# Pinning the layernorms of the first two sequences ahead of the sums, in a transformer block on one Trainium2 core

## Chip, core and metric

The kernel runs on one core of a Trainium2 chip. A core has five engines with their own instruction queues: TensorE (matmuls, "PE" in the profile), VectorE ("DVE"), ScalarE ("ACT"), GpSimd ("POOL") and SyncE ("SP", which here only starts DMAs). Each works through its queue in order and waits on semaphores for the others. The metric is the device time of one execution in microseconds (us), the median of several runs.

## What is computed

Sixteen sequences of 512 tokens with 256 features, all in float32. Each is layernormed; then linear attention with 16 heads and a mixture of experts are both applied to the normed tokens, and all is added to the input:

```python
xn = (x - mean) / sqrt(var + 1e-5)
q, k, v = xn @ Wq + bq, xn @ Wk + bk, xn @ Wv + bv
q, k = elu(q) + 1, elu(k) + 1
kv = einsum('bkhd,bkhm->bhdm', k, v)
attn = (q . kv) / max(q . sum(k), 1e-6) @ Wo + bo
shared = swiglu(xn @ w_in.T) @ w_out.T
h = swiglu(xn @ w1.T)
# 2 groups of 4 experts; softmax in the best group, two best experts e
routed = sum over the two: w_e * (h @ w2[e].T)
out = x + attn + shared + routed
```

## The kernel before

A sequence is four tiles of 128 tokens. For each sequence the kernel makes the layernorm `xn`, its transpose `xnT`, the keys together with the routing's logits (`pk`, 266 columns), the queries (`pq`), the feature maps of both, the sum of keys (`k2`, `ksb`), `pxk` (the product of normed tokens and keys, from which `mix` makes the attention's matrix `kvo`), the two SwiGLU hidden layers (`phr`, `hr` in token rows for the experts; `phs`, `hs` in columns for the shared part), and the output `po`. Sequence 0 computes the SwiGLU products directly (`first_rows`, `first_hidden`); the later ones with seven products in place of eight (`seven`). Rows for the experts go to DRAM (`h_d`). After the last sequence the tokens, sorted by pairs of experts, are read back by indirect DMAs and multiplied by the pair's weights (`Tiles`); this takes from about 792 us to the end.

The loop over sequences runs ahead: in the pass for sequence b, `front(b + 1)` computes keys, queries, feature maps and routing of b + 1, `normalize(b + 2)` the layernorm of b + 2, and `x` of b + 3 is loaded. Layernorms of sequences 0 and 1 are transposed on TensorE and copied out of PSUM by ScalarE; those of later sequences go through DRAM and VectorE's 32x32 transposes (`turn`, `qT` and `xnT`).

Three things set the order of the instructions. A scheduler puts each engine's instructions in an order by its own estimate of times. `tc.keep_in_program_order` (called `pin` in `first`) keeps an instruction in the order in which the program names it, among the pinned ones of its engine. `tc.issue_after(ins)` puts instructions of the same engine as `ins` behind it.

PSUM holds eight tiles: six of the pool `ps_mm` (tag `mm`: `pt`, `pk`, `pxk`, `phr`, `phs`, `pvk`, `pm`) and two of `ps_y` (`py`: the first queries, key sums, `po`). TensorE cannot begin a product until an earlier tile's slot was read and so freed, by VectorE or ScalarE. In both kernels the slot of `phs` of block 1 of sequence 0 is the one that `hr` of tile 1 frees.

Names and lines used below:

- L327 to L331: statistics, reciprocal and scale of sequence 0's layernorm (VectorE), L329 its Sqrt (ScalarE); L285 to L292 the same in `normalize`, for the others.
- L336/L339 and L302/L305: the transposes of sequences 0 and 1 on TensorE, and ScalarE's copies.
- L343: keys and queries of sequence 0; L404 and L415: keys and queries of the others. L369/L370 and L408/L409 add the biases to keys (`kk`) and logits (`lg`), L372 and L419 to queries (`qq`); the change calls the first pair `keep`.
- L382: `res`, the sums x + bo, on GpSimd; L668/L669: GpSimd's sum of keys; L507: `ahead_of`, its running counts for the routing.
- L389 to L394: the feature map (min, Exp, and the combining step on VectorE).
- L643, L661: the SwiGLU products of sequence 0 (`hr`, `hs_all`); L519: the weight sums made between them; L559 to L576: the seven-product form.
- L724 to L731: the normalizer `qk`, `rz`, and the scaled queries, stored to `q_d` (L736).
- L703/L708: `vk`; L713: `pm`.

Of the kernel before, what the change touches and what calls it, by code (L numbers as in the profile page):

```python
# [10 lines left out]
FP = mybir.dt.float32  # L11
AF = mybir.ActivationFunctionType
ALU = mybir.AluOpType
AX = mybir.AxisListType

P = 128
# [5 lines left out]
def block_kernel(  # L22
# [29 lines left out]
    nc = tc.nc  # L52
    B, S, D = x.shape
# [5 lines left out]
    KD = D // P  # L59
    KH = HID // P  # L60
    NT = S // P
# [22 lines left out]
    keep = ctx.enter_context(tc.tile_pool(name="keep", bufs=1))  # L84
    work = ctx.enter_context(tc.tile_pool(name="work", bufs=2))
    one = ctx.enter_context(tc.tile_pool(name="one", bufs=1))
    small = ctx.enter_context(tc.tile_pool(name="small", bufs=2))
    dram = ctx.enter_context(tc.tile_pool(name="dram", bufs=1, space=bass.MemoryType.DRAM))
    ps_mm = ctx.enter_context(tc.tile_pool(name="ps_mm", bufs=6, space=bass.MemoryType.PSUM))
# [10 lines left out]
    x_all, kk_all, qq_all, xn_all = (  # L100
        keep.tile([P, 2, NT, D], FP, name=f"{n}_all") for n in ("x", "kk", "qq", "xn")
    )
# [22 lines left out]
    eps_sb = const.tile([P, 1], FP)  # L125
    nc.gpsimd.memset(eps_sb, LN_EPS)
    ident = const.tile([P, P], FP)
    make_identity(nc, ident)

    xs = {0: load_x(0, NT)}  # L130
# [26 lines left out]
    for q in range(NQ):  # L157
        nc.gpsimd.dma_start(
            out=bv_sb[ts(q, Q)], in_=bv[ts(q, KD * Q)].rearrange("(c i) -> i c", i=Q)
# [22 lines left out]
    for k in range(KD):  # L182
        for c in range(KD):
            nc.sync.dma_start(
                out=wv_sb[:, k, ts(c, P)].rearrange("p (q i) -> p q i", i=Q), in_=by_quadrant(wv[ts(k, P), :])[:, c]
            )
    wo_sb = wp.tile([P, KD, D], FP)
    for q in range(NQ):
        nc.sync.dma_start(
            out=wo_sb[ts(q, Q)], in_=wo[ts(q, KD * Q), :].rearrange("(c i) d -> i c d", i=Q)  # L190
# [4 lines left out]
    def load_expert(i):  # L195
# [13 lines left out]
        out=headmask, in_=ones, pattern=[[-DH, P // DH], [0, DH]],  # L209
# [3 lines left out]
        out=headmask, in_=headmask, pattern=[[DH, P // DH], [0, DH]],  # L213
# [5 lines left out]
        out=before, in_=ones, pattern=[[1, P]],  # L219
# [3 lines left out]
    place = const.tile([P, NT * G, EG], FP)  # L223
# [28 lines left out]
    last_xn, last_copy = [], []  # L252
# [18 lines left out]
    def normalize(b):  # L271

        xt = xs[b]
        st = small.tile([P, NT, 6], FP, tag="st", name=f"st_{b}")
        mv = small.tile([P, NT, 2], FP, tag="mv", name=f"mv_{b}")
        sd = small.tile([P, NT], FP, tag="sd", name=f"sd_{b}")
        rs = small.tile([P, NT], FP, tag="rs", name=f"rs_{b}")
        xn = xn_all[:, b % 2]

        n = 1 if b == 0 else NT  # L280
        made = []
        for g in range(0, NT, n):
            with tc.issue_after(last_xn[-1].ins) if last_xn else nullcontext():
                for t in range(g, g + n):
                    nc.vector.bn_stats(out=st[:, t, :], in_=xt[:, t, :])  # L285
            for t in range(g, g + n):
                nc.vector.bn_aggr(out=mv[:, t, :], in_=st[:, t, :])
            with tc.issue_after(last_copy[-1].ins) if last_copy else nullcontext():
                nc.scalar.activation(sd[:, g : g + n], mv[:, g : g + n, 1], AF.Sqrt, bias=eps_sb)
            nc.vector.reciprocal(rs[:, g : g + n], sd[:, g : g + n])  # L290
            for t in range(g, g + n):
                made.append(nc.vector.tensor_scalar(  # L292
                    xn[:, t, :], xt[:, t, :], mv[:, t, 0:1], rs[:, t : t + 1],
                    ALU.subtract, ALU.mult,
                ))
        last_xn[:] = made[-1:]
        xnT = work.tile([P, KD, S], FP, tag="xnT", name=f"xnT_{b}")
        if b < 2:
            for t in range(NT):
                pt = ps_mm.tile([P, KD, P], FP, tag="mm", name=f"pt_{b}_{t}")  # L300
                for c in range(KD):
                    nc.tensor.transpose(  # L302
                        pt[:, c, :], xn[:, t, :].rearrange("p (m c) -> p c m", c=KD)[:, c], ident
                    )
                last_copy.append(nc.scalar.copy(xnT[:, :, ts(t, P)], pt))  # L305
            return xn, xnT, None
        last_copy.clear()
        nc.sync.dma_start(out=xn_d[b % 2].rearrange("(t p) d -> p t d", p=P), in_=xn)
        return xn, xnT, turn(xnT, xn_d[b % 2], "xb", b, "(i c)")

    def first():

        pin = tc.keep_in_program_order
        xt, xn, kk, qq = xs[0], xn_all[:, 0], kk_all[:, 0], qq_all[:, 0]
        st = small.tile([P, NT, 6], FP, tag="st", name="st_0")
        mv = small.tile([P, NT, 2], FP, tag="mv", name="mv_0")
        sd = small.tile([P, NT], FP, tag="sd", name="sd_0")  # L320
        rs = small.tile([P, NT], FP, tag="rs", name="rs_0")
        lg = small.tile([P, NT, E + G], FP, tag="lg", name="lg_0")
        xnT = work.tile([P, KD, S], FP, tag="xnT", name="xnT_0")
        pks, pqs = [], []

        def place(t):
            pin(nc.vector.bn_stats(out=st[:, t, :], in_=xt[:, t, :]))  # L327
            pin(nc.vector.bn_aggr(out=mv[:, t, :], in_=st[:, t, :]))
            pin(nc.scalar.activation(sd[:, t : t + 1], mv[:, t, 1:2], AF.Sqrt, bias=eps_sb))  # L329
            pin(nc.vector.reciprocal(rs[:, t : t + 1], sd[:, t : t + 1]))  # L330
            last_xn[:] = [pin(nc.vector.tensor_scalar(  # L331
                xn[:, t, :], xt[:, t, :], mv[:, t, 0:1], rs[:, t : t + 1], ALU.subtract, ALU.mult
            ))]
            pt = ps_mm.tile([P, KD, P], FP, tag="mm", name=f"pt_0_{t}")
            for c in range(KD):
                pin(nc.tensor.transpose(  # L336
                    pt[:, c, :], xn[:, t, :].rearrange("p (m c) -> p c m", c=KD)[:, c], ident
                ))
            last_copy[:] = [pin(nc.scalar.copy(xnT[:, :, ts(t, P)], pt))]  # L339

        def times(to, t, w):
            for k in range(KD):
                pin(nc.tensor.matmul(  # L343
                    to, lhsT=xnT[:, k, ts(t, P)], rhs=w[:, k, :], start=(k == 0), stop=(k == KD - 1)
                ))

        def keys(t):
            pks.append(ps_mm.tile([P, KR], FP, tag="mm", name=f"pk_0_{t}"))
            times(pks[t], t, wkr_sb)

        def queries(t):
            if t % 2 == 0:
                pqs.append(ps_y.tile([P, 2, D], FP, tag="py", name=f"pq_0_{t}"))
            times(pqs[-1][:, t % 2, :], t, wq_sb)

        place(0)
        place(1)
        keys(0)
        keys(1)
        queries(0)  # L360
        place(2)
        queries(1)
        keys(2)
        place(3)
        keys(3)
        queries(2)
        queries(3)
        for t in range(NT):
            pin(nc.vector.tensor_tensor(kk[:, t, :], pks[t][:, 0:D], bkr_sb[:, 0:D], ALU.add))  # L369
            pin(nc.vector.tensor_tensor(lg[:, t, :], pks[t][:, D:KR], bkr_sb[:, D:KR], ALU.add))  # L370
        for i, pq in enumerate(pqs):
            nc.vector.tensor_tensor(  # L372
                qq[:, 2 * i : 2 * i + 2, :], pq, bq_sb.unsqueeze(1).to_broadcast([P, 2, D]), ALU.add
            )
        return xn, xnT, (qq, kk, lg)

    def residual(b):

        res = work.tile([P, NT, BASE], FP, tag="res", name=f"res_{b}")
        xt = xs.pop(b)  # L380
        for t in range(NT):
            nc.gpsimd.tensor_tensor(res[:, t, 0:D], xt[:, t, :], bo_sb, ALU.add)  # L382
        return res

    def feature_map(b, y, tag):

        low = one.tile([P, NT, D], FP, tag="low", name=f"{tag}_{b}")
        if tag == "km":
            nc.vector.tensor_scalar(low, y, 0.0, None, ALU.min)  # L389
            nc.scalar.activation(low, low, AF.Exp)  # L390
        else:
            nc.scalar.activation(low, y, AF.Relu, scale=-1.0)
            nc.scalar.activation(low, low, AF.Exp, scale=-1.0)
        nc.vector.scalar_tensor_tensor(y, y, 0.0, low, ALU.max, ALU.add)  # L394

    def project(b, xnT):

# [582 lines left out]

    waiting = list(range(G * NL))

    *normed_0, (qq, kk, lg) = first()
    normed = {0: (*normed_0, None), 1: normalize(1)}
    res = residual(0)
    feature_map(0, kk, "km")
    feature_map(0, qq, "qm")
    route(0, lg, res)
    fronts = {0: (res, qq, kk)}
    queries = {}  # L990
    xs[2] = load_x(2)
    for b in range(B):
        xn, xnT, _ = normed.pop(b)
        res, qq, kk = fronts.pop(b)
        if b + 1 < B:
            fronts[b + 1] = front(b + 1, normed[b + 1][1])
        if b + 2 == B:

            nc.sync.dma_start(
                out=h_d[ts(b + 1, S), HID:ROW].rearrange("(t p) h -> p t h", p=P), in_=fronts[b + 1][0]  # L1000
# [43 lines left out]
    n = nc.values_load(  # L1044
        filled, min_val=TT, max_val=TILES,
        skip_runtime_bounds_check_because="whole tiles for all tokens, a part of a tile more for a pair",
    )
# [31 lines left out]
    for half, queue in enumerate((nc.sync, nc.scalar)):  # L1079
# [4 lines left out]
        for j in range(2):  # L1084
            t = 2 * half + j
# [36 lines left out]
```

## Time and profile before

| | |
|---|---|
| median of 3 runs | 1045.91 us (1045.9 to 1046.4) |
| the profiled execution | 1045.97 us; span from first to last instruction 1044.2 us |
| TensorE's mean granted clock | 0.992 |
| TensorE idle from 0 to 60 us | 10.4 us |
| TensorE idle from 60 to 735 us | 3.9 us |
| ScalarE: loads of an activation table | 46, at 1.28 us |

The profile is of one execution. Times in its rows are us from the start of the span, unless marked ns; "x4" counts instructions. In a row in order of time the first two numbers are start and duration, and a bracket at its end says how long the engine stood idle before it and what ended that. In a table of windows each engine has its busy time and number of instructions; after them stand TensorE's granted clock (1.00 is full speed), the share of the DMA engines, and GB/s. Matmuls overlap, so their starts, not their durations, give the pace. A float32 matmul of the program is two instructions on TensorE.

### The profile page before, as it was taken

The numbers are of one execution on the slowest core, as the hardware profiler recorded it, in microseconds if no ns is written. First come the engines' busy times: TensorE is split into PE (matmuls) and PEld (weight loads), VectorE is DVE, ScalarE is ACT, GpSimd is POOL, SyncE is SP. The second block draws the span as 40 slices with busy tenths as digits, with TensorE's granted clock in tenths as the row PEclk, the third lists the DMA queues.
The fourth block names the chain that finished last, engine by engine and source line by source line (L and its number), as shares of the span: only waits on it lengthen the run. The fifth ranks groups of instructions, "written<-read, shape, count | busy, mean of one in ns | idle before, by whom it ended". The sixth has DMA issues, their size and how long they took to land. (4 is left out here: it accounts for less than half of the span.)

```text
span 1044.2 us, 12410 instructions
## 1 busy us (share of the span) xinstructions
PE 1011.8 (97%) x3704; PEld 685.2 (66%) x3704; DVE 787.8 (75%) x1976; ACT 479.1 (46%) x886; POOL 242.3 (23%) x353
## 2 busy tenths in 40 slices
PE   6999999999999999999999999999896999999998
PEld 4566868677786868686777768686672444444445
DVE  5969797978788797878786877868975666666662
ACT  2415353534344352535344443425138666667770
POOL 5202020110202021110202020211022555565541
PEclk9999999999999999999999999999998999999999
DMA  7142624425151523314141313221253445544441
GB/s 217 42 138 87 174 87 116 127 71 151 51 161 49 162 78 87 121 42 141 41 121 56 115 57 114 84 61 61 60 141 127 142 137 154 160 149 149 149 125 69
DMA packets 130436, 114.24 MB, mean 109 GB/s; under 512 B 72605, under 2 KB 114589, under 8 KB 130368
## 3 DMA queue, kind: packets, MB, share of 16 engines
q1 hardware_dynamic: 120080, 77.42, 25.3%
q0 software_dynamic: 8912, 35.21, 11.2%
q10 hardware_dynamic: 1376, 0.80, 0.3%
q8 instruction: 31, 0.51, 0.2%
q14 instruction: 37, 0.30, 0.1%
HBM read 63.52 MB, written 50.27 MB: 109 GB/s over the span
## 5 line engine op out<-in xcount | busy, mean ns | idle before, releaser
L952 PE MATMUL py<-w_sb,hT 128*128 x536 | 233.1, 598 | 8.4 <-DMA w_sb<-in_w 8.4
L952 PEld LDWEIGHTS py<-w_sb,hT 128*128 128x128 f32 x536 | 102.7, 192 | 137.7 <-issue 137.7
L750 PE MATMUL po<-wout_sb,hs_all 128*128 128x256 f32 x512 | 124.9, 382 | 1.9 <-DVE hs_all L572 1.4
L382 POOL TENSOR_TENSOR res<-x_all,bo_sb 128x256 f32<-128x256 f32 x64 | 49.0, 796 | 271.7 <-DMA h_d<-res 204.9
L750 PEld LDWEIGHTS po<-wout_sb,hs_all 128*128 128x128 f32 x512 | 95.8, 191 | 17.4 <-DVE hs_all L572 3.4
L965 POOL DMA_INDIRECT out<-y,goal x67 | 67.8, 1012 | 104.3 <-DVE y L962 95.1
L761 DVE TENSOR_TENSOR res<-po,res 128x256 f32<-128x256 f32 x60 | 25.5, 424 | 74.7 <-PE po L750 72.0
L668 POOL TENSOR_TENSOR k<-kk_all 128x512 f32<-128x512 f32 x16 | 20.9, 1309 | 261.8 <-DVE sm L450 251.9
L750 PE MATMUL po<-kvo,qT 128*128 128x256 f32 x256 | 65.9, 383 | 0.0
L587 PE MATMUL phr_w<-w_sb,ss 128*128 128x512 f32 x120 | 62.2, 600 | 3.6 <-DVE hr L566 2.2
L613 PE MATMUL phs_w<-ss,win_sb 128*128 128x256 f32 x240 | 61.6, 379 | 0.0
L613 PE MATMUL phs_t<-xnT,win_sb 128*128 128x256 f32 x240 | 61.6, 379 | 0.0
L587 PE MATMUL phr_t<-w_sb,xnT 128*128 128x512 f32 x120 | 61.3, 593 | 0.0
L404 PE MATMUL pk<-wkr_sb,xnT 128*128 128x266 f32 x240 | 58.9, 395 | 0.3 <-ACT xnT L305 0.3
L613 PE MATMUL phs_t<-ss,win_sb 128*128 128x256 f32 x240 | 59.1, 379 | 0.0
L587 PE MATMUL phr_t<-w_sb,ss 128*128 128x512 f32 x120 | 59.0, 593 | 0.0
L390 ACT ACTIVATE km<-km 128x1024 f32<-128x1024 f32 x16 | 16.9, 1058 | 90.7 <-DVE km L389 90.7
L681 PE MATMUL pxk<-kk_all,xn_all 128*128 128x256 f32 x256 | 57.9, 379 | 0.0
L923 ACT COPY hb<-qq_all 32x256 f32<-32x256 f32 x108 | 43.4, 402 | 26.2 <-DMA qq_all<-h_d,source 22.8
L415 PE MATMUL pq<-w_sb,xnT 128*128 128x256 f32 x240 | 54.2, 379 | 0.0
L750 PEld LDWEIGHTS po<-kvo,qT 128*128 128x128 f32 x256 | 47.5, 190 | 8.9 <-ACT kvo L717 3.0
L681 PEld LDWEIGHTS pxk<-kk_all,xn_all 128*128 128x128 f32 x256 | 48.6, 190 | 6.6
(215 smaller groups left out, 1936.3 us busy)
## 6 DMA issues: line engine op xcount, KB each, us to landing
h_d<-hr SPq DMA_DIRECT2D x64, 256.0 KB, 2.4
q_d<-qq_all SPq DMA_DIRECT2D x16, 512.0 KB, 2.8
qb<-q_d SPq DMA_DIRECT2D x64, 128.0 KB, 3.0
w_sb<-in_w SPq DMA_DIRECT2D x64, 128.0 KB, 3.5
h_d<-res SPq DMA_DIRECT2D x60, 129.0 KB, 1.9
x_all<-in_x SPq DMA_DIRECT2D x15, 512.0 KB, 5.3
xn_d<-xn_all SPq DMA_DIRECT2D x14, 512.0 KB, 3.5
xb<-xn_d SPq DMA_DIRECT2D x56, 128.0 KB, 3.0
```

The costliest lines, as they stand in the source:

```text
L382: nc.gpsimd.tensor_tensor(res[:, t, 0:D], xt[:, t, :], bo_sb, ALU.add)
L404: nc.tensor.matmul(pk, lhsT=xnT[:, k, ts(t, P)], rhs=wkr_sb[:, k, :], start=(k == 0), stop=(k == KD - 1),)
L415: nc.tensor.matmul(pq[:, t, :], lhsT=xnT[:, k, ts(t2 + t, P)], rhs=wq_sb[:, k, :], start=(k == 0), stop=(k == KD - 1),)
L587: tc.keep_in_program_order(nc.tensor.matmul(to, lhsT=xs7[i][:, ts(u, P)], rhs=w1_in[W7[i]], start=start, stop=stop, skip_group_check=True,))
L613: tc.keep_in_program_order(nc.tensor.matmul(split(to)[:, f, :], lhsT=win_in[W7[i]][:, ts(2 * u + f, P)], rhs=xs7[i], start=start and f == ...
L668: nc.gpsimd.tensor_tensor(k2, kk[:, 0:2, :], kk[:, 2:4, :], ALU.add)
L681: nc.tensor.matmul(pxk[:, c, :], lhsT=xn[:, t, ts(c, P)], rhs=kk[:, t, :], start=(t == 0), stop=(t == NT - 1),)
L750: step = nc.tensor.matmul(po, lhsT=a, rhs=w, start=(i == 0), stop=(i == len(parts) - 1))
L761: nc.vector.tensor_tensor(res[:, t, 0:D], po, res[:, t, 0:D], ALU.add)
L923: nc.scalar.copy(there[ts(q, Q), a - near, 0:n, :], self.hg[ts(a, Q), 0:n, ts(q, W)])
L952: nc.tensor.matmul(py.rearrange("p j d -> p (j d)"), lhsT=self.hT[:, f, ts(j, P)], rhs=w2_sb[:, f, bass.ds(regs[i % TR], 2 * D)], start=(f ...
L965: stored = nc.gpsimd.indirect_dma_start(out=out_rows, out_offset=bass.IndirectOffsetOnAxis(ap=self.goal[:, i : i + 1], axis=0), in_=y, in_ ...
```

## The change

In `first`, which writes out sequence 0's start by hand, the layernorms of sequences 0 and 1 are now both made, pinned, and split into three steps: `measure` (statistics), `scale` (Sqrt, reciprocal, the normed tokens) and `place` (transposes and ScalarE's copy). Sequence 0's tiles are measured and scaled one by one; each transposition is named one tile later than its layernorm. Keys of tiles 1 to 3 follow the last transposition, and then all queries. The additions of keys and logits (`keep`) of tiles 0 and 1 stand ahead of sequence 1's statistics, those of tiles 2 and 3 behind them, and the scale and transposition of sequence 1 behind those. `normalize` loses its part for the first two sequences and serves sequences 2 and later. `feature_map` returns its last instruction, and `residual(0)` is called inside `tc.issue_after` of the one that queries of sequence 0 return.

```diff
+        def measure(b, t):
+            st, mv, _, _ = stats[b]
+            pin(nc.vector.bn_stats(out=st[:, t, :], in_=xs[b][:, t, :]))
+            pin(nc.vector.bn_aggr(out=mv[:, t, :], in_=st[:, t, :]))
+
+        def scale(b, t, n):
+            _, mv, sd, rs = stats[b]
+            pin(nc.scalar.activation(sd[:, t : t + n, 0], mv[:, t : t + n, 1], AF.Sqrt, bias=eps_sb))
+            pin(nc.vector.reciprocal(rs[:, t : t + n], sd[:, t : t + n]))
+            for i in range(t, t + n):
+                last_xn[:] = [pin(nc.vector.tensor_scalar(
+                    xn_all[:, b, i, :], xs[b][:, i, :], mv[:, i, 0:1], rs[:, i], ALU.subtract, ALU.mult
+                ))]
+
+        def place(b, t):
+            pt = ps_mm.tile([P, KD, P], FP, tag="mm", name=f"pt_{b}_{t}")
             for c in range(KD):
                 pin(nc.tensor.transpose(
...
-        place(0)
-        place(1)
-        keys(0)
-        keys(1)
-        queries(0)
-        place(2)
-        queries(1)
-        keys(2)
-        place(3)
-        keys(3)
-        queries(2)
-        queries(3)
-        for t in range(NT):
+        def keep(t):
             pin(nc.vector.tensor_tensor(kk[:, t, :], pks[t][:, 0:D], bkr_sb[:, 0:D], ALU.add))
             pin(nc.vector.tensor_tensor(lg[:, t, :], pks[t][:, D:KR], bkr_sb[:, D:KR], ALU.add))
+
+        for t in range(NT):
+            measure(0, t)
+            scale(0, t, 1)
+            if t:
+                place(0, t - 1)
+        keys(0)
+        place(0, NT - 1)
+        for t in range(1, NT):
+            keys(t)
+        for t in range(NT):
+            queries(t)
+        for t in range(2):
+            keep(t)
+        for t in range(NT):
+            measure(1, t)
+        for t in range(2, NT):
+            keep(t)
+        scale(1, 0, NT)
+        for t in range(NT):
+            place(1, t)
         for i, pq in enumerate(pqs):
...
-        nc.vector.scalar_tensor_tensor(y, y, 0.0, low, ALU.max, ALU.add)
+        return nc.vector.scalar_tensor_tensor(y, y, 0.0, low, ALU.max, ALU.add)
...
-    *normed_0, (qq, kk, lg) = first()
-    normed = {0: (*normed_0, None), 1: normalize(1)}
-    res = residual(0)
+    first_xnT, (qq, kk, lg) = first()
+    normed = {b: (xn_all[:, b], first_xnT[b], None) for b in range(2)}
     feature_map(0, kk, "km")
-    feature_map(0, qq, "qm")
+
+    with tc.issue_after(feature_map(0, qq, "qm").ins):
+        res = residual(0)
     route(0, lg, res)
```

More of the change, by code (lines that the diff above doesn't have):

```diff
@@ L278, in normalize @@
         xn = xn_all[:, b % 2]
-        n = 1 if b == 0 else NT
         made = []
-        for g in range(0, NT, n):
+        for g, n in [(0, NT)]:
             with tc.issue_after(last_xn[-1].ins) if last_xn else nullcontext():
@@ L297, in normalize @@
         xnT = work.tile([P, KD, S], FP, tag="xnT", name=f"xnT_{b}")
-        if b < 2:
-            for t in range(NT):
[L300 to L306, printed above, removed]
         last_copy.clear()
@@ L316, in first @@
         pin = tc.keep_in_program_order
[L317 to L321, printed above, removed]
+        stats = []
+        for b in range(2):
+            stats.append([
+                small.tile([P, NT, n], FP, tag=tag, name=f"{tag}_{b}")
+                for tag, n in (("st", 6), ("mv", 2), ("sd", 1), ("rs", 1))
+            ])
@@ L322, in first @@
+        kk, qq = kk_all[:, 0], qq_all[:, 0]
         lg = small.tile([P, NT, E + G], FP, tag="lg", name="lg_0")
-        xnT = work.tile([P, KD, S], FP, tag="xnT", name="xnT_0")
+        xnT = [work.tile([P, KD, S], FP, tag="xnT", name=f"xnT_{b}") for b in range(2)]
         pks, pqs = [], []
-        def place(t):
-            pin(nc.vector.bn_stats(out=st[:, t, :], in_=xt[:, t, :]))
+        def measure(b, t):
+            st, mv, _, _ = stats[b]
+            pin(nc.vector.bn_stats(out=st[:, t, :], in_=xs[b][:, t, :]))
@@ L328, in place @@
             pin(nc.vector.bn_aggr(out=mv[:, t, :], in_=st[:, t, :]))
[L329 to L334, printed above, removed]
+        def scale(b, t, n):
[6 more added lines that the diff above has]
+                ))]
@@ L335, in place @@
+        def place(b, t):
+            pt = ps_mm.tile([P, KD, P], FP, tag="mm", name=f"pt_{b}_{t}")
             for c in range(KD):
                 pin(nc.tensor.transpose(
-                    pt[:, c, :], xn[:, t, :].rearrange("p (m c) -> p c m", c=KD)[:, c], ident
+                    pt[:, c, :], xn_all[:, b, t, :].rearrange("p (m c) -> p c m", c=KD)[:, c], ident
                 ))
-            last_copy[:] = [pin(nc.scalar.copy(xnT[:, :, ts(t, P)], pt))]
+            last_copy[:] = [pin(nc.scalar.copy(xnT[b][:, :, ts(t, P)], pt))]
@@ L343, in times @@
                 pin(nc.tensor.matmul(
-                    to, lhsT=xnT[:, k, ts(t, P)], rhs=w[:, k, :], start=(k == 0), stop=(k == KD - 1)
+                    to, lhsT=xnT[0][:, k, ts(t, P)], rhs=w[:, k, :], start=(k == 0), stop=(k == KD - 1)
                 ))
@@ L354, in queries @@
             times(pqs[-1][:, t % 2, :], t, wq_sb)
-        place(0)
-        place(1)
-        keys(0)
-        keys(1)
-        queries(0)
-        place(2)
-        queries(1)
-        keys(2)
-        place(3)
-        keys(3)
-        queries(2)
-        queries(3)
-        for t in range(NT):
+        def keep(t):
             pin(nc.vector.tensor_tensor(kk[:, t, :], pks[t][:, 0:D], bkr_sb[:, 0:D], ALU.add))
             pin(nc.vector.tensor_tensor(lg[:, t, :], pks[t][:, D:KR], bkr_sb[:, D:KR], ALU.add))
+        for t in range(NT):
[18 more added lines that the diff above has]
+            place(1, t)
         for i, pq in enumerate(pqs):
@@ L374, in first @@
             )
-        return xn, xnT, (qq, kk, lg)
+        return xnT, (qq, kk, lg)
     def residual(b):
```

## The prediction

> **What bounds the kernel now.** I read the page's busy table first, then TensorE's waits, then the start in order of time.
>
> ```profile
> PE 1011.8 (97%) x3704; PEld 685.2 (66%) x3704; DVE 787.8 (75%) x1976; ACT 479.1 (46%) x886; POOL 242.3 (23%) x353
> ```
>
> TensorE is busy for 97%. The change leaves its matmuls as they are, so it can only alter TensorE's idle time and its clock. The waits of TensorE (total us, times, longest):
>
> ```profile
> PE pt L336 <- DVE xn_all L331: 7.0, 2, 5.3
> ...
> PE phr_w L587 <- DVE hr L566: 2.2, 7, 0.3
> PE pt L302 <- DVE xn_all L292: 2.2, 1, 2.2
> ...
> PE phs L655 <- DVE hr L643: 0.4, 1, 0.4
> ```
>
> The first 5.3 us is the load of x and the first layernorm; it stays. The other three rows are the subject: sequence 1's transposes wait for its layernorm (L302), the first SwiGLU product waits for a freed sum tile (L655), and once per sequence phr_w waits for VectorE (L587). TensorE in order of time (start, us, count, wait before it):
>
> ```profile
> 17.29 1.89 PE L343 MATMUL pq<-w_sb,xnT 128*128 128x256 f32 x8
> 21.40 1.45 PE L302 MATMUL pt<-ident,xn_all 128*128 128x128 f32 x8 [2.22 <-DVE xn_all L292]
> 23.14 5.47 PE L404 MATMUL pk<-wkr_sb,xnT 128*128 128x266 f32 x16 [0.30 <-ACT xnT L305]
> ```
>
> Sixteen pk matmuls take 3.76 us at 76.60, but 5.47 here: the granted clock (last but two) was 0.50 from 23.1 to 26.4, after the gap.
>
> ```profile
> 24.00:25.00 1.00, 1.00 (x3) 0.76 (x3) 0.48 (x2) 0.05 (x1) 0.00 (x0) 0.50 0.05 15
> ```
>
> VectorE in order of time:
>
> ```profile
> 14.32 0.88 DVE L331 TENSOR_SCALAR xn_all<-x_all,mv,rs 128x256 f32<-128x256 f32 x1
> ...
> 24.52 1.08 DVE L285 BATCH_NORM_STATS2 st<-x_all 128x6 f32<-128x256 f32 x3 [2.12 <-DMA x_all<-in_x]
> ```
>
> ```profile
> 49.76 0.68 DVE L643 TENSOR_TENSOR hr<-phr,sa_hr 128x512 f32<-128x512 f32 x1
> ...
> 51.18 0.68 DVE L643 TENSOR_TENSOR hr<-phr,sa_hr 128x512 f32<-128x512 f32 x1
> ```
>
> From 24.52, when sequence 2's x lands, VectorE runs without a gap to past 51: it is nearly as late as TensorE. So TensorE's early loss is not simply to be won back.
>
> **Part 1: sequence 0.** TensorE's new order is three transposes, keys 0, the last transpose, keys 1 to 3, queries. Sqrt 1 now stands before copy 0 on ScalarE, so it starts at 5.74 (aggregate 5.52 to 5.70) and not 6.28. Tile 3's Sqrt is no longer behind a copy that waits for the slow products (3.95 us of VectorE before 14.12): its xn comes at about 9.7, not 15.1. The third transpose costs keys 0 some 0.5 us (8.13 to 8.65). [...]
>
> **Part 2: sequence 1's layernorm.** x1 lands at 3.66 + 7.3 = 10.96, so it hides. VectorE: two keeps to 13.45; four statistics with aggregates at 0.60 to 15.85; two keeps at 0.41 to 16.65; reciprocal and a query sum to 17.35. The Sqrt fits under the keeps. The four scales take 0.33 each alone, but while GpSimd's res sums run (13.63 to 19.22) one took 0.88 (row at 14.32): 1.3 to 2.6 us, the last at about 19.9. pk then starts at 20.15 instead of 23.14. The gap is broken by transposes, so I expect the clock to stay full: pk ends at 23.75, pq at 27.2, against 31.91. TensorE leads by 4.7 us.
>
> **Part 3: what takes it back.** VectorE stands at the statistics of x2 (SP issue 19.90, all its predecessors unchanged), where it arrives about 22.2 and waits to 24.52 as before. Behind it, in order, stand two kk/lg pairs and kk's map, so kk is ready at 24.52 + 0.34 + 0.41 + 0.34 + 0.34 + 1.14 = 27.1: just in time for pxk at 27.2. Of what stood behind this wait before, only one kk/lg pair (0.41) and one token sum (0.34) are now ahead of it. The built order puts hr of tile 0 some 8 us of work earlier (about 41), but between it and hr of tile 1 lie a weight sum 0.6, the rest of the routing 1.3, qq's map 1.14, qk 1.14, rz 1.7, x2's scales 1.3 and qq's product 1.14, with hr itself 0.6: some 9 us (starts in VectorE's order of time, 41.06 to 50.36). Up to there the two orders hold the same work, so tile 1's hr ends at 51.86 - 0.75 + 0.3 (another small operation behind k's sum) = 51.4. phs of block 1 needs that tile (both kernels). It began at 54.03 before:
>
> ```profile
> 50.49 1.98 PE L655 MATMUL phs<-xnT,win_sb 128*128 128x512 f32 x4 [0.37 <-DVE hr L643]
> ```
>
> (eight at 0.43 and the 0.1 of the restart). TensorE would arrive at 48.85, stands for 2.55 us, and keeps 54.03 - 51.45 = 2.6; vk, at about 64.75, cuts it to 2.15. [...] Another 2.2 us gap, at 824, left the clock full, so I take a value between, **1.7**; ends 0.5 and 2.6. SP's queue moves too: the store of hr 0 now stands ahead of q_d, which goes at about 50.2 (48.52 before), so qb lands near 58; its transpose comes after vk at 64.75. Nothing waits for it.
>
> **Part 4: GpSimd's sums.** issue_after orders only instructions on the engine of the one it names, VectorE; the sums are GpSimd's. In the built order they stand where they stood, with the same waits (x and bo). So: 0. Were they moved, VectorE would reach the x2 wait up to 1.3 us earlier: still 0.
>
> **Part 5: six later sequences.** The scheduler's clock has moved too, and with it sequences 2 to 8 (TensorE's order stays). Windows from pk to pk (us, then busy of PE, PEld, DVE, ACT, POOL):
>
> ```profile
> 76.60:124.03 47.43, 47.43 (x195) 35.91 (x194) 38.12 (x97) 21.37 (x31) 7.39 (x11) 1.00 0.44 123
> 124.03:171.95 47.92, 47.61 (x195) 35.97 (x194) 39.94 (x100) 20.12 (x30) 6.02 (x11) 1.00 0.40 110
> ...
> 500.18:547.94 47.76, 47.48 (x195) 35.94 (x194) 37.95 (x99) 20.29 (x31) 6.42 (x11) 1.00 0.29 89
> ```
>
> The first has no wait; the next six each carry the 0.31 of L587 and its restart. Its cause is GpSimd's res sums in the midst of the xn scales:
>
> ```profile
> 181.39 1.24 DVE L292 TENSOR_SCALAR xn_all<-x_all,mv,rs 128x256 f32<-128x256 f32 x1
> ```
>
> ```profile
> 183.29 2.88 POOL L382 TENSOR_TENSOR res<-x_all,bo_sb 128x256 f32<-128x256 f32 x4
> ```
>
> In the new order res comes behind ahead_of, where VectorE adds PSUM tiles, and ScalarE and VectorE follow the first window's pattern. VectorE was idle for 1.27 us before hr (94.01) there, and qT's transpose (1.15), which now precedes it, fits. So 6 x (47.93 - 47.43) = **2.9**; ends 0 and 3.0. The price is the table loads: 53 instead of 46. The first window has three ahead of r1:
>
> ```profile
> 86.78 1.28 ACT L393 ACT_TABLE_LOAD   x1
> 88.07 1.06 ACT L393 ACTIVATE qm<-qm 128x1024 f32<-128x1024 f32 x1
> 89.03 0.57 ACT L559 COPY r_phr<-phr_t 128x512 f32<-128x512 f32 x1
> ```
>
> The copy ends at 89.60, and TensorE adds onto that tile at 89.67. [...] The row has 1.28 and the next instruction at once, and the 47.43 includes it. I take the row: 0. The two more loads near sequence 0 lie in ScalarE's idle time (6.16 us before 50.53).
>
> **Sum.** The profiled execution took 1045.97 (span 1044.2 and 1.8 around it; the median is 1045.91, 0.06 less). 1.7 + 0 + 2.9 = 4.6: **1041.3**. From 200 to 719 VectorE waits for TensorE again and again, so a lead reaches the end; from sequence 10 on the orders are equal. [...]
>
> **Rivals.**
> - Only the start gains; L587's wait stays, because qT or another sum fills the place: 1045.9 - 1.7 = 1044.2. For it: VectorE is late by 0.3 only.
> - Only the sequences gain; the wait for hr and a cold clock eat the start: 1043.0.
> - **Slower:** ScalarE. The copy of r1 has 0.07 us to spare behind three loads; if a load, Sqrt or kk's map ends later there than in the first window, TensorE pays it six times. A whole load exposed: 6 x 1.28 = 7.7, less 1.7: 1051.9. It outweighs the start from 0.35 us a sequence. Against it: the first window.
> - Nothing: VectorE as late as before at 51.86, sequences unchanged: 1045.5.
>
> **How the numbers follow.** Forecast 0.60, only the start 0.18, only the sequences 0.11, slower 0.07, nothing 0.04. The range 1039.8 to 1044.3 takes in both partial cases. A measurement here tells 0.2% (2.1 us) from no change. Faster by more needs less than 1043.8: the forecast, most of the third case, a fifth of the second: 0.72; same 0.20; slower 0.08.
>
> **What would show it.** Right: pk of sequence 1 near 20 at full clock; bn of x2 still released by its DMA near 24.5; a wait of some 2.5 us of phs on hr near 49; res of sequence 0 still at 13.6; L587's waits gone and pk to pk 47.4 from sequence 3 to 9. Wrong: waits of phr on r1's copy, or the clock at half before 30.

## The result, and the profile after

The changed kernel took 1040.17 us (median of four runs, 1039.37 to 1040.75) beside 1046.16 (1045.9 to 1048.25) for the kernel before on the same chip: a ratio of 0.9938, 95% interval 0.9921 to 0.9955. It is faster by 6.0 us; 4.6 were forecast. Put on 1045.91, the ratio gives 1039.4, just below the predicted range (1039.8 to 1044.3). The profiled execution took 1039.37 us with a span of 1037.6, against 1045.97 and 1044.2.

Busy time of the engines:

```profile
PE 1007.8 (97%) x3704; PEld 683.3 (66%) x3704; DVE 777.7 (75%) x1976; ACT 488.1 (47%) x893; POOL 249.6 (24%) x353
```

The work is the same (3704 matmuls, 1976 VectorE instructions). ScalarE has 893 instructions, not 886: the seven more table loads. VectorE is busy for 10.1 us less with the same instructions, so some of them became shorter. TensorE's waits (total us, times, longest):

```profile
PE pt L335 <- DVE xn_all L328: 7.6, 5, 5.3
...
PE phs L663 <- DVE hr L651: 1.5, 1, 1.5
...
PE phr_w L595 <- DVE hr L574: 0.3, 1, 0.3
PE phs L663 <- ACT sa_hr L649: 0.2, 1, 0.2
```

(Lines after L394 of the kernel before are 8 or 9 higher here.) Of the three rows that the prediction was about, the 2.2 us before sequence 1's transposes shrank to 0.5 in two pieces, six of the seven 0.3 us waits of phr_w are gone, and a new wait of 1.5 us for hr came in. TensorE in order of time:

```profile
19.57 0.48 PE L335 MATMUL pt<-ident,xn_all 128*128 128x128 f32 x2 [0.32 <-DVE xn_all L328]
19.88 3.76 PE L412 MATMUL pk<-wkr_sb,xnT 128*128 128x266 f32 x16
...
50.87 1.98 PE L663 MATMUL phs<-xnT,win_sb 128*128 128x512 f32 x4 [1.52 <-DVE hr L651]
```

pk of sequence 1 starts at 19.88 and takes 3.76 us; the granted clock is 1.00 from 19.57 to 23.64. phs of block 1 starts at 50.87, and the clock stays at 1.00 from there to 73. VectorE in order of time:

```profile
16.79 2.63 DVE L328 TENSOR_SCALAR xn_all<-x_all,mv,rs 128x256 f32<-128x256 f32 x4
...
24.43 0.43 DVE L283 BATCH_NORM_STATS2 st<-x_all 128x6 f32<-128x256 f32 x1 [2.73 <-DMA x_all<-in_x]
...
40.96 0.68 DVE L651 TENSOR_TENSOR hr<-phr,sa_hr 128x512 f32<-128x512 f32 x1
...
50.13 0.68 DVE L651 TENSOR_TENSOR hr<-phr,sa_hr 128x512 f32<-128x512 f32 x1
```

VectorE stands for x2's load until 24.43, as before (24.52), and from there it runs without a gap to hr of tile 1. GpSimd in order of time, its sums with bo:

```profile
13.59 5.69 POOL L390 TENSOR_TENSOR res<-x_all,bo_sb 128x256 f32<-128x256 f32 x8 [4.17 <-DMA bo_sb<-in_bo]
```

They start at 13.59 (13.63 before). The instruction behind which `issue_after` was to put them, the last one of sequence 0's query map, on VectorE, starts 17 us later:

```profile
30.80 1.22 DVE L402 SCALAR_TENSOR_TENSOR qq_all<-qq_all,qm 128x1024 f32<-128x1024 f32 x1
```

So the half of the change that its description names last does not happen. The windows from pk to pk, two of them (us, then busy of PE, PEld, DVE, ACT, POOL):

```profile
120.94:168.38 47.44, 47.44 (x196) 35.98 (x195) 37.43 (x97) 21.31 (x31) 6.94 (x11) 1.00 0.40 112
...
494.10:541.86 47.76, 47.48 (x195) 35.94 (x194) 38.15 (x99) 20.29 (x31) 6.43 (x11) 1.00 0.29 89
```

The first was 47.92 long before with VectorE busy for 39.94; the second, in the stretch where both kernels have one order, is 47.76 in both.

**Where the 6.6 us of the span came from**, by the start of pk in the two traces: sequence 2 starts at 73.60 and not 76.60 (3.00); sequence 9 at 405.54 and not 411.62 (6.08, so 3.08 more); the last at 691.70 and not 697.78 (6.08). The other 0.5 us lies behind that. There the trace has TensorE's granted clock at 0.50 for 6.8 us from 783.4, where it was 10.2 us from 787.6 before; that this is its cause fits, but is not shown. The mean granted clock differs from run to run of one kernel, too (0.995, 0.995, 0.993 and 0.993 in the four of the changed one), and the medians, 6.0 apart, do not need this cause.

### The profile page after: what moved, and what is told of

Read it like the earlier page. It is cut to its first block, busy times and chain, and to the rows that moved or that the text cites. A ratio compares the mean times of both kernels' runs of the same rounds, so it can differ in the third digit from the quotient of the medians.

```text
span 1037.6 us, 12416 instructions
## 1 busy us (share of the span) xinstructions
PE 1007.8 (97%) x3704; PEld 683.3 (66%) x3704; DVE 777.7 (75%) x1976; ACT 488.1 (47%) x893; POOL 249.6 (24%) x353
```

## Experiments

All are timed in five rounds against the kernel before. Ratios have their 95% intervals; three groups ran on three chips, where the kernel before took 1046.88, 1045.9 and 1045.94.

### 1. GpSimd's sums put back, first attempt

```diff
+        with tc.issue_after(added[b - 2].ins) if 5 <= b < 11 else nullcontext():
             nc.gpsimd.tensor_copy(wins, place)
```

(`added[b]` is the last of sequence b's sums.)

> The changed kernel with GpSimd's sums with bo of sequences 3 to 8 put back where the kernel before has them: ahead of the copy of wins and of ahead_of, instead of behind ahead_of. Nothing else moves on any engine. Theory (the gain is two separate sums, 3.0 us at the start and 3.1 us in six sequences): phr_w waits again for VectorE once in each of six sequences, pk to pk goes from 47.43 back to 47.93, pk of sequence 2 still starts at 73.6, and the time is 1040.2 + 3.0 = 1043.2. Rival (the later sequences gain by VectorE's and ScalarE's new order, not by where GpSimd's sums stand): pk to pk stays at 47.43 and the time at 1040.2.

1040.4 us, 0.9941 (0.9929 to 0.9953); pk to pk stayed at 47.43. This looks like the rival, but the trace says that the edit missed. GpSimd in order of time:

```profile
135.61 2.28 POOL L517 TENSOR_TENSOR ahead_of<-ahead_of,hot 128x12 bf16<-128x12 bf16 x4 [2.78 <-DVE hot L500]
137.87 2.79 POOL L391 TENSOR_TENSOR res<-x_all,bo_sb 128x256 f32<-128x256 f32 x4
140.61 0.21 POOL L476 COPY wins<-place 128x32 f32<-128x32 f32 x1
```

Only wins went behind the sums; ahead_of passed both, and the sums stayed late. It tells nothing on the question; experiment 3 repeats it.

### 2. GpSimd's sums moved late in the kernel before, nothing else

```diff
         route(b, lg, res)
+        if 3 <= b < 9:
+            added[b, "sums"]()    # the four sums, issue_after the last ahead_of
```

> The kernel before with nothing changed but GpSimd's sums with bo of sequences 3 to 8, moved behind ahead_of; no pins, no other order on any engine. Theory (where these sums stand is the whole of the later gain): the six waits of phr_w go, pk to pk falls from 47.93 to 47.43 six times, pk of sequence 2 still starts at 76.6, and the time is 1045.9 - 3.0 = 1042.9. Rival (the new order of VectorE and ScalarE is needed as well): 1045.9, or a part of the 3.0.

1042.23 us, 0.9961 (0.9949 to 0.9973): by the ratio 4.1 us less, with no instruction moved on any engine but GpSimd. A window:

```profile
123.74:171.09 47.35, 47.35 (x195) 36.05 (x194) 38.13 (x100) 20.12 (x30) 5.92 (x11) 1.00 0.40 112
```

The six waits are gone and the six intervals are 47.35, 0.58 less each: 3.5 us. pk of sequence 2 started at 76.31. So where these sums stand is enough by itself.

### 3. GpSimd's sums really put back

```diff
+            with tc.issue_after(added[b].ins) if 3 <= b < 9 else nullcontext():
                 nc.gpsimd.tensor_tensor(ahead_of[:, t + 1, :], ahead_of[:, t, :], hot[:, t, :], ALU.add)
```

with the edit of experiment 1.

> The changed kernel with GpSimd's sums with bo of sequences 3 to 8 really put back: behind the sums of k and ahead of ahead_of and wins, as in the kernel before (in the first attempt they stayed behind ahead_of). Orders of VectorE, ScalarE and TensorE untouched. Theory (the sums beside VectorE's scales make hr late; in the changed order hr has about 0.9 us to spare and the sums cost VectorE 1.3 to 1.8): phr_w waits again in each of six sequences, 0.4 to 0.9 us each, time 1040.2 + 2 to 5, so 1042.5 to 1045. Rival (VectorE's new order alone hides it): no waits, 1040.2.

1045.41 us, 0.9990 (0.9981 to 0.9999): almost the whole gain of the change is lost, 5.2 us against 1040.17. The gain of the start is still there (pk of sequence 2 at 73.78); the six sequences are now slower than in the kernel before, 48.30 and not 47.93. GpSimd, VectorE and TensorE in order of time, in one of the six sequences:

```profile
132.57 2.89 POOL L391 TENSOR_TENSOR res<-x_all,bo_sb 128x256 f32<-128x256 f32 x4
```

```profile
132.57 0.88 DVE L291 TENSOR_SCALAR xn_all<-x_all,mv,rs 128x256 f32<-128x256 f32 x1
133.37 0.71 DVE L480 TENSOR_TENSOR wins<-wins,beats 128x24 f32<-128x24 f32 x1
134.00 0.87 DVE L291 TENSOR_SCALAR xn_all<-x_all,mv,rs 128x256 f32<-128x256 f32 x1
134.79 0.70 DVE L481 TENSOR_TENSOR wins<-wins,beats 128x24 f32<-128x24 f32 x1
135.42 0.40 DVE L291 TENSOR_SCALAR xn_all<-x_all,mv,rs 128x256 f32<-128x256 f32 x1
```

```profile
141.04 1.12 PE L598 MATMUL phr_w<-w_sb,ss 128*128 128x512 f32 x2 [0.58 <-DVE hr L577]
```

While GpSimd sums (132.57 to 135.46), a scale takes 0.87 and not 0.40, and an operation on 128x24 takes 0.70. In the changed kernel the same operation is

```profile
132.71 0.17 DVE L478 TENSOR_TENSOR wins<-wins,beats 128x24 f32<-128x24 f32 x1
```

VectorE loses about 2 us, and hr comes 0.58 us late for TensorE. The rows show VectorE slow for as long as GpSimd sums; by what GpSimd holds it up, no run here shows.

The four kernels give a table of two by two, in us from pk to pk (sequences 3 to 9):

| | VectorE and ScalarE ordered as before | ordered as after |
|---|---|---|
| GpSimd's sums early | 47.93 | 48.30 |
| GpSimd's sums late | 47.35 | 47.44 |

The late sums are worth 0.58 and 0.86; the new order of VectorE and ScalarE by itself costs 0.37 and 0.09. Where the 0.09 arises the trace shows. ScalarE and TensorE of the changed kernel:

```profile
130.05 1.06 ACT L400 ACTIVATE qm<-qq_all 128x1024 f32<-128x1024 f32 x1 [1.33 <-DVE kk_all L402]
131.12 1.28 ACT L401 ACT_TABLE_LOAD   x1
132.42 1.06 ACT L401 ACTIVATE qm<-qm 128x1024 f32<-128x1024 f32 x1
133.38 0.57 ACT L567 COPY r_phr<-phr_t 128x512 f32<-128x512 f32 x1
```

```profile
134.02 1.10 PE L595 MATMUL phr_t<-w_sb,ss 128*128 128x512 f32 x2
134.96 1.02 PE L595 MATMUL phr_w<-w_sb,ss 128*128 128x512 f32 x2
```

The product that adds onto r1's tile takes 1.10 and not 1.02: the copy ends at 133.95, just too late, although that is 0.07 before the start in the product's row. In experiment 2 ScalarE has no table load there (none between 128.72 and 142.77), and pk to pk is 47.35.

### 4. TensorE's gap filled, in the kernel before

```diff
+                if b == 1 and t == 0:
+                    for i in range(18):
+                        tc.keep_in_program_order(nc.tensor.transpose(pt[:, i % KD, :], ident, ident))
```

> The kernel before with 18 more transposes of the identity on TensorE in the 2.2 us gap before sequence 1's transposes, so that the clock stays full and pk of sequence 1 takes 3.76 instead of 5.47 us. They write the tile that the first true transpose then overwrites. Theory (VectorE bounds the start: the sum tile of hr 0 is freed at 50.4 whatever TensorE does): TensorE is 1.7 us earlier at 26 and waits 1.7 us longer, some 2.1, for hr at 49; time 1045.9, within 0.5. Rival (the half clock is lost time): 1.7 us gained, 1044.2.

1046.28 us, 0.9993 (0.9984 to 1.0002): no gain, as expected. TensorE in order of time:

```profile
18.46 2.13 PE L303 MATMUL pt<-ident 128*128 128x128 f32 x18
...
22.58 3.86 PE L407 MATMUL pk<-wkr_sb,xnT 128*128 128x266 f32 x16 [0.30 <-ACT xnT L308]
...
51.42 1.98 PE L658 MATMUL phs<-xnT,win_sb 128*128 128x512 f32 x4 [2.43 <-DVE hr L646]
```

pk took 3.86 us and not 5.47 (3.76 at a granted clock of 1.00), and all of it was given back in the wait for hr, 2.43 in place of 0.37. phs even starts 0.93 later than before (51.42 against 50.49): in this execution x2's load ended VectorE's wait at 25.43 and not 24.52, and hr moved with it.

### 5 and 6. x2's load ahead of wo and wout, in the kernel before; then both

```diff
-    for q in range(NQ):
-        nc.sync.dma_start(out=wo_sb[ts(q, Q)], ...)
...
     xs[2] = load_x(2)
+    for q in range(NQ):
+        tc.keep_in_program_order(nc.sync.dma_start(out=wo_sb[ts(q, Q)], ...))
```

(wout's load moves with them.)

> The kernel before with the load of sequence 2's x issued ahead of those of wo and wout; no other instruction moves on any engine. Theory (in the kernel before two late things stand side by side, VectorE's wait for x2 and TensorE's slow pk of sequence 1, and taking one away brings only what the other leaves): VectorE then waits for pk instead, hr of tile 0 comes some 0.7 us earlier, TensorE's wait of 0.37 us at 50.5 goes and no more: 1045.9 - 0.4 = 1045.5. Rival (the load alone sets the start): 2.1 us gained, 1043.8.

> The kernel before with both: the load of x2 ahead of wo and wout, and 18 transposes of the identity in TensorE's gap, so that the clock stays full. Each alone was expected or measured at 0 to 0.4 us. Theory (two bounds side by side): together they bring 1.7 to 2.2 us at the start, 1044.0. Rival (something else makes hr of tile 0 late): the sum of the two, 0.4, 1045.5.

The load alone: 1045.67 us, 0.9994 (0.9985 to 1.0003). Load and filled gap: 1043.6, 0.9978 (0.9970 to 0.9987), 2.3 us less. Each alone brings nothing that can be told; both together do. But the margins are wide: by their ratios the two alone add up to 1.4 us, with a margin of about as much, so the times do not show that both together bring more than the sum. What shows that one hides behind the other is experiment 4's wait of 2.43 us, which is gone with both. For the load alone the trace is less plain:

```profile
22.43 5.01 PE L399 MATMUL pk<-wkr_sb,xnT 128*128 128x266 f32 x16
...
48.79 1.88 PE L650 MATMUL phs<-xnT,win_sb 128*128 128x512 f32 x4
```

phs starts 1.70 earlier than before, without a wait. Of that, 1.17 is TensorE's own: pk of sequence 1 started 0.71 earlier in this execution and took 0.46 less (5.01 against 5.47). Only the other 0.5 is the wait for hr, 0.37, and its restart. TensorE with both:

```profile
23.22 3.86 PE L402 MATMUL pk<-wkr_sb,xnT 128*128 128x266 f32 x16 [0.30 <-ACT xnT L303]
...
48.42 1.89 PE L653 MATMUL phs<-xnT,win_sb 128*128 128x512 f32 x4
```

phs starts at 48.42 and waits for nothing (50.49 before).

### 7. x2's load earlier, in the changed kernel

The edit of experiment 5.

> The changed kernel with the load of sequence 2's x issued ahead of the five loads of wo and wout on SP's queue, not behind them. Theory (VectorE's 2.7 us wait for this load is what makes hr of tile 1 late): x lands some 3 us earlier, VectorE's wait at 24.4 shrinks to under 0.5, hr of tile 1 ends before 49.3, TensorE's 1.5 us wait of phs goes and vk comes earlier too: 1040.2 - 1.5 = 1038.7. Rival (the wait moves on, to vk, kk or another load): 1040.2.

1038.3 us, 0.9917 (0.9904 to 0.9931): the fastest kernel here by its median, 1.9 us under the changed one (the intervals of the two ratios just overlap). VectorE:

```profile
21.62 0.43 DVE L278 BATCH_NORM_STATS2 st<-x_all 128x6 f32<-128x256 f32 x1 [0.31 <-DMA x_all<-in_x]
```

The statistics of x2 start 2.8 us earlier, hr of tile 1 ends before 46.1, and TensorE's waits for it are gone; pk of sequence 2 starts at 71.88. What is left is 0.24 us before pm, for vk. The scheduler also moved some of VectorE's instructions here, hr of tile 1 among them, so not all of it is the load.

### 8. hr of tile 1 ahead of other work, in the changed kernel

```diff
+            with tc.high_priority() if t == 1 else nullcontext():
                 nc.vector.tensor_tensor(hr, both[1], sa, ALU.mult)
```

> The changed kernel with hr of tile 1 given priority on VectorE, so that it stands 2.2 us of work earlier. Theory (VectorE has no slack up to vk: vk is ready at 63.9 and pm starts at 64.0): TensorE no longer waits for hr, reaches pm 1.5 us earlier and waits there for vk: 1040.2, gain at most 0.2. Rival (hr is the only late product): 1.5 us gained, 1038.7.

1039.65 us, 0.9938 (0.9924 to 0.9951): no gain that can be told from the changed kernel's 0.9938. TensorE:

```profile
63.04 0.70 PE L759 MATMUL po<-wout_sb,hs_all 128*128 128x256 f32 x2 [0.50 <-DVE hs_all L670]
64.61 0.70 PE L722 MATMUL pm<-wo_sb,vk 128*128 128x256 f32 x2 [0.88 <-DVE vk L717]
```

The wait of phs went, and 0.50 and 0.88 came in at po and pm. VectorE is the bound up to vk; a new order of its work only moves the wait.

### 9. hr of tile 1 later, in the changed kernel

```diff
+            for _ in range(2 if t == 1 else 1):
                 nc.vector.tensor_tensor(hr, both[1], sa, ALU.mult)
```

> The changed kernel with the product for hr of tile 1 computed a second time, behind hr of tile 2, so that TensorE waits 2.7 us for it instead of 1.5: the length of wait that the prediction expected here. [...] By the row of the kernel before (2.2 us were enough for 3.4 us at half clock) a half-clock interval follows: 1.2 + 1.2 to 1.7 more, 1042.6 to 1043.1.

1041.09 us, 0.9949 (0.9935 to 0.9962), 0.9 us more than the changed kernel, though the intervals of the two ratios overlap. TensorE:

```profile
52.41 1.98 PE L664 MATMUL phs<-xnT,win_sb 128*128 128x512 f32 x4 [2.12 <-DVE hr L652]
```

The wait came out at 2.1, not 2.7, and the products behind it come 0.43 us apart up to 63.70, as they do in the changed kernel at a clock of 1.00: no half clock there. pk of sequence 2 starts at 75.20, 54.83 after pk of sequence 1, where it was 53.72: 1.1 later.

### 10. Sequence 1's layernorm without pins

```diff
-        for t in range(NT):
-            measure(1, t)
...
-        scale(1, 0, NT)
-        for t in range(NT):
-            place(1, t)
```

and `normalize(1)` with its transposes as in the kernel before.

> The changed kernel with the pins of sequence 1's layernorm taken away, so that only sequence 0's layernorm, transposes and products have the new pinned order; GpSimd's sums stay as in the changed kernel. Theory A (sequence 1's pins bring the start): the 3.1 us of the six sequences stay and the 3.0 us of the start go, 1043.2. Theory B (the new order of sequence 0 sets it all, and sequence 1's layernorm finds its place by itself): pk of sequence 1 starts near 20, and the time is 1040.2 or up to 1 us more.

1039.07 us, 0.9922 (0.9910 to 0.9935): not slower than the changed kernel. pk of sequence 1 starts at 20.75, that of sequence 2 already at 71.96, and phs waits for no hr. VectorE:

```profile
32.24 0.41 DVE L283 BATCH_NORM_STATS2 st<-x_all 128x6 f32<-128x256 f32 x1
```

The scheduler here puts x2's statistics at 32.24, long after the load has landed, so VectorE never stands for it. The first interval between pk's is 48.05 and not 47.35, which takes 0.7 of this back.

### 11. GpSimd's sums of sequences 0 and 1 really moved

```diff
-    with tc.issue_after(feature_map(0, qq, "qm").ins):
+    feature_map(0, qq, "qm")
+    mark = small.tile([P, 1], FP, tag="mark", name="mark")
+    with tc.issue_after(nc.gpsimd.tensor_copy(mark, qq[:, 0, 0:1]).ins):
         res = residual(0)
```

> The changed kernel with GpSimd's sums with bo of sequences 0 and 1 really moved behind sequence 0's feature maps, by a one-column copy on GpSimd that reads the finished query map. The prediction's value for this: 0, 1040.2. Rival (the load of x2 must wait until sequence 0's sums have read x, so it is issued near 35 us in place of 19.8 and lands near 40, where VectorE's statistics of x2 now stand): VectorE waits some 1 to 3 us before hr of tile 1, and 1 to 2 us are lost, 1041.2 to 1042.2.

1040.72 us, 0.9948 (0.9935 to 0.9961): 0.5 us above the changed kernel, within what its runs scatter. SP's queue and VectorE:

```profile
32.68 0.39 SPq L110 DMA_DIRECT2D x_all<-in_x  x1
```

```profile
40.21 0.41 DVE L283 BATCH_NORM_STATS2 st<-x_all 128x6 f32<-128x256 f32 x1
```

x2's load is 13 us later, as the rival said, but the scheduler also put its statistics at 40.21, and no wait for the load remains. The profiled run was the slowest of five (1043.81): TensorE waits 1.22 us for sa_hr, 0.7 in two pieces at po and 0.8 at pm, and the mean granted clock was 0.992, where the four others have 0.993 to 0.995. Whether the move costs a few tenths stays open.

## Why the prediction was off, point by point

**Part 1, sequence 0: right.** Sqrt 1 started at 5.73 (5.74) and tile 3's xn came at 9.95 (9.7). The queries' last product ended at 17.9, where it was 19.18.

**Part 2, sequence 1's layernorm: right.** pk started at 19.88 (20.15) with the clock at 1.00, behind scales that took 2.63 us beside GpSimd (1.3 to 2.6). But experiment 10 adds that sequence 1's pins aren't needed for it; the new order of sequence 0 brings it.

**Part 3, what takes it back: the mechanism was right, its size wrong, and here is most of the miss.** VectorE did wait for x2 (24.43 against 24.52), and TensorE stood at phs of block 1 for hr of tile 1. The start was put at 1.7, at most 2.6, and measured 3.0. This is the step that failed: too much was taken back from TensorE's lead. Three terms of that sum were off:
- *tile 1's hr ends at 51.86 - 0.75 + 0.3 = 51.4.* It ended at 50.81, and phs started at 50.87 and not 51.45: 0.6 more. From x2's statistics to that end VectorE was busy for 27.17 us with 102 instructions before, and 26.27 with 99 after. The three fewer are the kk/lg pair and the token sum that I counted; from start to start they took 0.86 us, for my 0.75, and x2 came 0.09 earlier. The 0.3 added for another small operation behind k's sum is what did not come. Beside GpSimd's sums of k of sequence 1 (37.3 to 39.5 in both) other operations stretched after than before, but in all by no more:

```profile
37.44 1.23 DVE L444 TENSOR_TENSOR ex<-lg,mx 128x8 f32<-128x8 f32 x1
...
38.82 0.92 DVE L530 TENSOR_TENSOR ss<-xnT 128x256 f32<-128x256 f32 x1
```

```profile
37.58 1.05 DVE L467 TENSOR_TENSOR pe<-ex,sm 128x32 f32<-128x32 f32 x1
...
38.95 0.53 DVE L478 TENSOR_TENSOR wins<-wins,beats 128x24 f32<-128x24 f32 x1
```

- *vk, at about 64.75, cuts it to 2.15.* vk was ready at 63.94 and pm started at 64.00 with no wait shown, so the cut of 0.45 did not come. It was close: in experiment 8, where TensorE came earlier, pm waited 0.88.
- *I take a value between, 1.7.* No run shows this term: the clock was 1.00 behind the wait (50.87 to 73), so this other 0.45 was not lost either, and the start brought 3.0.

These make 1.5; 0.16 was lost again on the way to pk of sequence 2 and gives the measured 3.0 (2.6 + 0.6 = 3.16 at phs).

On the clock, the products behind waits of 1.52, 2.12 and 2.43 us (changed kernel, experiments 9 and 4) come 0.43 us apart, the pace that goes with a clock of 1.00. At two other places the kernel before has gaps of nearly one length. Behind the 2.22 us in front of sequence 1's transposes the clock was 0.50 from 23.03 to 26.45 and pk took 5.47 us; behind the same wait it took 5.20 and 5.01 in experiments 2 and 5. Around the 2.17 us in front of pm at 825.91 the clock was 1.00 (820 to 831):

```profile
825.91 1.10 PE L713 MATMUL pm<-wo_sb,vk 128*128 128x256 f32 x4 [2.17 <-DVE vk L708]
```

```profile
824.00:827.00 3.00, 1.09 (x5) 1.02 (x6) 2.92 (x9) 1.55 (x4) 0.98 (x1) 1.00 0.67 214
```

So the length of a gap alone doesn't tell when the clock falls. I took the first of the two over to a place with other work behind the gap; that this makes the difference was not shown, and what decides stays open.

**Part 4, GpSimd's sums: right that they don't move,** for the reason given. The side remark on moving them missed x2's load, which must wait for sequence 0's sums (experiment 11); the value 0 held within the scatter.

**Part 5, six later sequences: right, 3.08 for 2.9** (6 x (47.93 - 47.43) is 3.0), and by the named cause: experiments 2 and 3 move nothing but GpSimd's sums and turn the wait off and on. Two of its steps were too smooth. The new order of VectorE and ScalarE is no help but a cost, which the late sums more than pay. And the slower rival's place was real at its smallest size: r1's copy does come late behind the table load, by 0.08 us. I read 0.07 to spare, but the first window of the kernel before has the same stretched product:

```profile
89.67 1.10 PE L587 MATMUL phr_t<-w_sb,ss 128*128 128x512 f32 x2
```

So the 47.43 that I took as the aim held this loss already, and the price of 0 came out only because of that. The load itself cost what its row said: under experiment 3 it starts 0.01 us behind the activation ahead of it, takes 1.28, and the next one starts 0.02 later. (That rival outweighs a start of 1.7 from 0.28 us a sequence, not 0.35.)

**The end:** the profiled pair differs by 0.5 us there, with the clock at 0.50 for 6.8 us and for 10.2.

## What to carry to other kernels

Where two engines are late at the same place, a test that relieves one of them can measure nothing (0.6 and 0.3 us alone here, neither clear of noise, and 2.3 together), so relieve both, and look at the waits, before you call either harmless. What a long elementwise run on GpSimd costs hung here on what VectorE did at that moment: four sums of 0.7 us cost TensorE 0.6 to 0.9 us in each sequence or nothing, by a shift of some 5 us. And with a scheduler in between, look at the built order of each engine before believing an experiment: one edit here moved something other than what it named, and half of the change moved nothing.

## What was not expected of the hardware

How far a small operation stretches beside GpSimd: 128x4 elements took 1.27 us on VectorE (0.15 otherwise), for the length of GpSimd's sum of keys:

```profile
27.13 0.15 DVE L464 TENSOR_TENSOR gm<-ex 128x4 f32<-128x4 f32 x1
27.20 1.27 DVE L465 TENSOR_TENSOR gm<-ex 128x4 f32<-128x4 f32 x1
```

```profile
27.13 1.33 POOL L676 TENSOR_TENSOR k<-kk_all 128x512 f32<-128x512 f32 x1 [7.86 <-DVE kk_all L402]
```

It ends at 28.47, with GpSimd's instruction at 28.46. And idle time of TensorE at one length went with a clock of 0.50 at one place (2.22 us, from 23.03 to 26.45) and of 1.00 at another (2.17 us, from 820 to 831), as told above.
